# A graph-attention kernel on one core: the fourth unit of tile 0 joined to the third by VectorE, the folds of one unit moved from GpSimd to VectorE, and a new order

## The chip, the cores and the metric

The kernel runs on one core of a Trainium2 chip. The metric is the device time of one launch in microseconds (us). The kernel before has a median of 1622.75 us over three runs (1618.98 to 1625.38); one more execution was profiled.

The engines are named as the profile names them: PE is TensorE's matmuls and PEld its weight loads, DVE is VectorE, ACT is ScalarE, POOL is GpSimd, SP is SyncE, which only issues DMAs here. A small q behind a name is the engine's sequencer. L1356 is line 1356 of the kernel.

## The reference

One layer of masked attention over a graph, behind a layer norm. `x` has 16 batches of 1024 rows of 512 numbers, `adj` is one 1024 x 1024 matrix for all batches, and there are 8 heads of 64.

```python
h = jnp.maximum(_layernorm(x, axis=-1), 0.0)
q = (h @ Wq + bq).reshape(b, n, H, HD)          # k and v likewise
scores = jnp.einsum('bihd,bjhd->bhij', q, k) / jnp.sqrt(jnp.float32(HD))
mask = jnp.where(adj == 0, jnp.float32(-1000000000.0), jnp.float32(0.0))
scores = scores + mask[None, None, :, :]
weights = jax.nn.softmax(scores, axis=-1)
out = jnp.einsum('bhij,bjhd->bihd', weights, v)
x = x + out.reshape(b, n, H * HD)
```

All of it is fp32. The inputs' `adj` is sparse, with few long rows and many short ones, so most scores are masked.

## The kernel before, in words

**The gather.** The kernel doesn't compute the masked scores. Once, at the start, it sorts the 1024 rows by their number of neighbours and makes for each row a list of its neighbours. The sorted rows form eight tiles of 128 rows (one row in a partition): tile 0 has the longest lists, up to 11 neighbours, tile 7 the shortest, 2 (`CAPS`). Rows with still more neighbours have the rest in "pieces" of four, 128 pieces in one tile of their own, called -1. For each batch the kernel computes k and v of all rows, stores them in DRAM (`store_kv`), and gathers for each slot of a list the k and v rows with one indirect DMA that GpSimd issues (L1288). A row's own k and v come with a direct DMA by SyncE instead (L1286, "own rows").

**Units.** A tile's slots are worked off in units of two to four slots, 14 a batch. Their numbers: 0 is tile 7, 1 tile 6, 2 tile 5 (written (5, 0): tile and first slot), 3 tile 4, 4 and 5 tile 3, 6 and 7 tile 2, 8 and 9 tile 1. Tile 0 has four: unit 10 is (0, 0), unit 11 the pieces (-1, 0), unit 12 (0, 4), unit 13 (0, 8) with three slots. A unit has one of six buffers (`g`) from its first gather to its last use, and the buffers go round in the units' order. In each unit:

- VectorE multiplies the gathered k by the query, which is in PSUM (`multiply`, L1298), and adds up each head (`score`, L1302);
- ScalarE takes the exponential (`exponent`, L1306);
- the v rows are weighted by it, most slots on ScalarE (`weigh_s`, L1332: eight small instructions, one for each head), one of some units on VectorE (`weigh_v`, L1318);
- the weighted slots are added together by `fold` (L1337), on VectorE or GpSimd. Of four slots the first step adds two slots to two and the second one to one; of three slots both steps add one to one. `fold_on_pool` sends a step of one slot to GpSimd if the unit is listed in `POOL_FOLDS`.

Units of the tiles 1 to 7 end on VectorE: `join` (L1344) adds the second unit of a tile to its first, and `scale` (L1392) or the shared weights divide by the sum of the exponentials. Tile 0 is added up on TensorE: `add_up` (L1356) multiplies what the folds left with the identity (`ident`), for the pieces with a matrix that gives each piece to its row (`owner_t`), all into one PSUM tile. In fp32 one such call is two matmul instructions in the profile. `residual` adds x (L1406), and GpSimd issues the scattered store (`put_out`, L1409).

**The other half.** For the next batch, in between: `load_x`, `stats`, `power`, `norm`, transposes on TensorE (`flip`) and copies by ScalarE (`unflip`), the projections (`proj_kv` and `queries`, L1057: four calls or eight instructions each), and their evictions by ScalarE (L1075) or VectorE (L1073). The queries of tile 0 are also copied by ScalarE to SBUF (`copy_q`, L1279), from where TensorE makes the pieces' queries (L1275).

**What sets the order.** Each engine runs its instructions in the order in which they are written. `planned` lists every operation with its engine, the operations before it and the buffers it uses; `PLACES` has a place for each (once, for the first k and v, for batches 0, 1, 2, for all from 3 on, for the last but one and for the last), to which `PERIOD` times the batch is added. `ordered` sorts each engine's queue by place and merges the queues. Waits are then put in by the data and buffers that the instructions share. In the last batch the units come in the order `LAST_ORDER`, tile 0 first, and other lists say which engine does what.

Of the kernel before, what the change touches and what calls it, by code (L numbers as in the profile page):

```python
# [57 lines left out]
UNITS = tuple(unit for t in TILES for unit in PARTS[t])  # L58
# [8 lines left out]
POOL_FOLDS = ((5, 0), (4, 0), (1, 0), (1, 4), (-1, 0))  # L67
# [6 lines left out]
LAST_BY_VECTOR = {(2, 0): 0, (2, 3): 0, (0, 0): 0, (-1, 0): 0, (3, 0): 0, (1, 4): 0}  # L74
VECTOR_RESIDUAL = (4,)
LAST_VECTOR_RESIDUAL = (5, 4, 6, 7)
# [21 lines left out]
        list_of=(-13.2, -13.4, 13.93, 14.05, -4.33, -7.76, -9.88, 14.25,),  # L98
        tell=(-12.63, -16.97, -13.14, 9.24, 0.89, 16.11, 17.75, 19.88,),
        spread=(45.38, 47.45, 30.7, 45.48, 45.35, 30.46, 22.54, 45.26,),  # L100
        collect=(-9.17, 5.02,),
        others=(14.42,),
        perm_of=(0.42,),
        spots=(26.84,),
        long_rows=(30.4,),
        long_blocks=(16.58, 20.59, 22.61, 24.22, 24.98,),
        longest=(27.18, 29.37, 32.28, 35.43, 36.11, 39.52, 41.52, 44.79, 45.14,),
        count_pieces=(46.89,),
        first_piece=(122.72,),
        owners=(94.07,),  # L110
        flip_owners=(136.43,),
        copy_owners=(113.68,),
        list_pieces=(137.27,),
        pieces=(127.38,),
        slots=(142.24,),
        add_bias=(-19.2, -17.6,),
        spread_bias=(68.07,),
        copy_bias=(89.7,),
# [4 lines left out]
        norm=(75.49, 76.09, 77.09, 77.49, 79.89, 80.09, 80.34, 80.69,),  # L123
        flip=(75.49, 75.69, 76.49, 76.69, 78.69, 78.89, 90.39, 104.64,),
        unflip=(75.89, 76.49, 77.29, 77.89, 80.49, 80.72, 96.22, 97.88,),
        proj_kv=(75.89, 77.49, 76.29, 77.89, 76.89, 78.49, 79.09, 79.29, 86.87, 98.15, 99.79, 107.75, 135.06, 147.6, 153,
            148.32,),
        evict_kv=(76.89, 79.29, 77.69, 79.49, 78.09, 80.29, 80.4, 80.66, 96.1, 96.13, 96.42, 106.28, 154.55, 162.49, 169.71,
            172.46,),
        store_kv=(78.35, 116.17, 119.38, 125.35, 140.7, 146.55, 148.18, 147.06,),  # L130
        variance=(75.89, 76.89, 79.29, 81.69,),
        power=(75.69, 76.29, 78.29, 87.8,),
# [3 lines left out]
        load_x=(30.09, 30.5, 38.8, 45.21, 45.44, 47.92, 49.07, 49.69,),  # L136
        norm=(2.13, 2.31, 24.77, 49.09, 71.39, 77.14, 77.27, 78.66,),
        flip=(50.32, 51.95, 54.11, 55.9, 60.64, 67.45, 67.52, 68.48,),
        unflip=(27.69, 53.06, 72.64, 77.2, 79.54, 81.13, 82.77, 84.23,),
        queries=(67.49, 69.07, 115.56, 126.07, 127.49, 138.29, 148.67, 168.76, 169.97,),  # L140
        gather=(45.09, 65.92, 63.96, 81.66, 82.98, 67.8, 87.05, 86.63, 69.01, 87.14, 102.98, 103.26, 67.61, 108.86, 109.63,
            108.64, 107.92, 79.49, 116.69, 119.1, 130.36, 131.45, 130.44, 102.76, 142.21, 138.67, 142.4, 144.98, 150.63,
            142.37, 142.46, 108, 152.91, 152.09, 152.7, 153.37, 153.1, 152.82, 153.23, 171.08, 171.84, 155.19, 172.79,
            155.41, 171.17, 171.11,),
        multiply=(47.46, 64.59, 81.01, 107.03, 126.74, 113.33, 126.77, 141.63, 149.43, 155.18, 163.45, 170.22, 180.88,
            178.07,),
        score=(47.54, 67.41, 96.06, 111.76, 129.2, 117.87, 128.06, 146.83, 153.31, 155.84, 165.66, 174.39, 181.78, 195.93,),
        exponent=(92.19, 93.82, 105.44, 111.15, 115.51, 115.42, 115.56, 141.97, 143.4, 152.67, 166.31, 172.53, 173.27,
            183.23,),
        row_sums=(64.37, 70.18, 97.04, 118.27, 142.77, 160.52, 163.48, 203.64,),  # L150
        share=(64.49, 74.75, 101.56, 119.16,),
        weigh_v=(69.44, 130.54, 142.01, 144.6, 161.03, 163.57, 170.25, 175.36, 195.82,),
        weigh_s=(92.85, 101.83, 100.44, 95.75, 106.78, 112.94, 106.75, 115.48, 115.39, 115.45, 122.29, 116.89, 121.19, 119.7,
            142.94, 135.53, 142.97, 143.03, 144.58, 154.99, 152.31, 153.27, 163.13, 166.52, 165.91, 171.8, 172.93, 171.74,
            173.08, 173.04, 172.99, 174.92, 175.62, 181.86, 185.22, 185.42, 187.44,),
        fold=(71.91, 97.01, 97.07, 132.47, 137.68, 138.95, 141.69, 143.23, 145.64, 143.05, 153.79, 155.15, 156.82, 161,
            163.76, 171.2, 173.85, 175.66, 181.17, 186.5, 187.92, 183.84, 200, 202.21, 204.35, 204.53,),
        residual=(109.25, 124.53, 138.45, 141.77, 153.19, 171.14, 178.55, 219.35,),
        put_out=(129.95, 130.51, 141.35, 142.43, 153.4, 178.16, 179.5, 225.23,),
        join=(147.89, 161.06, 175.01,),  # L160
        scale=(148.16, 161.67, 176.53, 211.41,),
        copy_q=(145.23,),
        add_up=(188.54, 194.88, 203.87, 205.55,),
        more=(201.41,),
# [212 lines left out]
PAIRED = ()  # L377
# [1230 lines left out]
```

## Time and profile before

| | |
|---|---|
| median of three runs (lowest, highest) | 1622.75 us (1618.98, 1625.38) |
| profiled execution: its time, its span | 1612.02 us, 1609.9 us |
| mean granted TensorE clock | 0.992 |
| busy, share of the span: PE, DVE, ACT, POOL | 98%, 94%, 90%, 78% |
| DMA: moved, mean over the span | 531.56 MB, 330 GB/s |
| L1356, sums of tile 0 on TensorE: with `ident`, with `owner_t` | 170 and 38 matmul instructions |
| L1337, folds: on VectorE, on GpSimd | 301 and 90 |
| L1344, joins on VectorE | 45 |
| L1406, residuals: on GpSimd, on VectorE | 109 and 19 |

Busy time is the union of an engine's instructions. The shares are means over a start (the sorting and the first batch, to about 100 us), a steady part, and the last batch (from about 1500 us). A wait is written as who waited, "<-", and what came last of what it waited for; the releaser is inferred.

### The profile page before, as it was taken

How to read it: one execution, taken by the hardware profiler on the slowest of the kernel's cores; microseconds unless marked ns; L12 is line 12 of the kernel's file. 1: busy time of each engine (PE TensorE's matmuls, PEld its weight loads, DVE VectorE, ACT ScalarE, POOL GpSimd, SP SyncE). 2: the span in 40 equal slices, each digit the busy share in tenths (PEclk: the TensorE clock that was granted, in tenths of full speed). 3: DMA queues.
4: the chain of work that ended last, by engine and by line, in shares of the span. 5: the costliest groups of instructions: out<-in, count | busy, mean ns of one | idle time of the engine just before them, and what ended most of it. 6: DMA issues, size and time to landing. Idle time of an engine off the chain costs nothing. (4 is left out here: it accounts for less than half of the span.)

```text
span 1609.9 us, 19515 instructions
## 1 busy us (share of the span) xinstructions
PE 1572.1 (98%) x4242; PEld 732.0 (45%) x4242; DVE 1518.2 (94%) x2075; ACT 1444.8 (90%) x5428; POOL 1258.7 (78%) x1185
## 2 busy tenths in 40 slices
PE   8999999999999999999999999999999999999687
PEld 4444444444444444444444444444444444444233
DVE  8889999999999999999999999999999999999897
ACT  4459999898999989899898989999998998989897
POOL 3777778887788888888788787878788887786666
PEclk9999999999999999999999999999999999999899
DMA  6499989999999999999999999999999999998886
GB/s 249 141 351 341 334 319 358 329 366 323 341 333 345 366 333 357 325 351 349 339 357 346 345 337 345 344 343 352 330 339 331 341 373 326 338 335 330 324 306 217
DMA packets 149876, 531.56 MB, mean 330 GB/s; under 512 B 19052, under 2 KB 19052, under 8 KB 149752
## 3 DMA queue, kind: packets, MB, share of 16 engines
q0 software_dynamic: 109840, 390.70, 67.9%
q1 hardware_dynamic: 39912, 139.56, 23.0%
q8 instruction: 35, 0.57, 0.1%
q14 instruction: 89, 0.73, 0.1%
HBM read 429.46 MB, written 100.72 MB: 329 GB/s over the span
## 5 line engine op out<-in xcount | busy, mean ns | idle before, releaser
L1332 ACT ACTIVATE g<-g,weights 128x64 f32<-128x64 f32 x4704 | 1160.3, 338 | 40.9 <-DVE weights L1311 37.8
L1288 POOL DMA_INDIRECT g<-kv,index x608 | 642.2, 1056 | 206.7 <-issue 163.2
L1057 PE MATMUL pq<-wq,hT 128*128 128x512 f32 x1024 | 462.4, 595 | 0.0
L1057 PE MATMUL pk<-wk,hT 128*128 128x512 f32 x960 | 431.7, 593 | 0.0
L1057 PE MATMUL pv<-wv,hT 128*128 128x512 f32 x960 | 431.4, 593 | 0.0
L1302 DVE TENSOR_REDUCE weights<-g 128x32 f32<-128x2048 f32 (+2 forms) x224 | 423.7, 1897 | 2.0
L1298 DVE TENSOR_TENSOR g<-g,pq 128x2048 f32<-128x2048 f32 (+2 forms) x208 | 388.7, 1870 | 28.1 <-DMA g<-kv 9.9
L1057 PEld LDWEIGHTS pq<-wq,hT 128*128 128x128 f32 x1024 | 195.8, 191 | 216.9 <-issue 213.2
L1057 PEld LDWEIGHTS pv<-wv,hT 128*128 128x128 f32 x960 | 182.4, 190 | 213.5 <-issue 210.6
L1057 PEld LDWEIGHTS pk<-wk,hT 128*128 128x128 f32 x960 | 182.7, 190 | 201.4 <-issue 196.8
L1337 DVE TENSOR_TENSOR g<-g 128x512 f32<-128x512 f32 (+1 forms) x301 | 253.9, 851 | 9.8 <-ACT g L1332 8.4
L1409 POOL DMA_INDIRECT out_dram<-x,perm x128 | 136.7, 1068 | 39.8 <-issue 30.6
L1002 POOL DMA_INDIRECT x<-in_x_dram,perm x128 | 135.8, 1061 | 34.9 <-issue 32.5
L1337 POOL TENSOR_TENSOR g<-g 128x512 f32<-128x512 f32 x90 | 115.0, 1284 | 17.6 <-DVE g L1337 10.5
L1037 ACT ACTIVATE h<-x,shift,rstd 128x512 f32<-128x512 f32 x120 | 96.5, 807 | 12.0 <-DVE shift L1027 11.4
L1318 DVE TENSOR_TENSOR g<-g,weights 128x512 f32<-128x512 f32 x143 | 101.9, 716 | 1.1 <-ACT weights L1306 0.6
L1356 PE MATMUL acc<-g,ident 128*128 128x512 f32 x170 | 84.4, 612 | 14.6 <-ACT g L1332 10.8
L1044 PEld LDWEIGHTS pht<-ident,h 128*128 128x128 f32 x512 | 63.2, 141 | 68.6 <-issue 52.7
L1406 POOL TENSOR_TENSOR x<-x,o 128x512 f32<-128x512 f32 x64 | 81.9, 1280 | 9.4 <-DVE o L1392 5.0
L1049 ACT COPY hT<-pht 128x512 f32<-128x512 f32 x128 | 73.0, 571 | 16.3 <-PE pht L1044 16.2
L1011 DVE BATCH_NORM_STATS2 st<-x 128x6 f32<-128x512 f32 x120 | 81.2, 677 | 1.6 <-DMA x<-in_x_dram,perm 1.6
L1044 PE MATMUL pht<-ident,h 128*128 128x128 f32 x512 | 76.5, 273 | 3.2 <-ACT hT L1049 1.9
(242 smaller groups left out, 1080.2 us busy)
## 6 DMA issues: line engine op xcount, KB each, us to landing
g<-kv SPq DMA_DIRECT2D x128, 512.0 KB, 7.7
kv<-kvt SPq DMA_DIRECT2D x120, 512.0 KB, 6.9
g<-kv,index POOLq DMA_INDIRECT x608, 6.9
adj<-in_adj_dram SPq DMA_DIRECT2D x8, 512.0 KB, 8.2
x_first<-in_x_dram SPq DMA_DIRECT2D x8, 256.0 KB, 6.0
x<-in_x_dram,perm POOLq DMA_INDIRECT x128, 5.5
out_dram<-x,perm POOLq DMA_INDIRECT x128, 6.6
wk<-in_L_gnn_Wk_dram SPq DMA_DIRECT2D x1, 1024.0 KB
```

The source lines that it names most:

```text
L1002: nc.gpsimd.indirect_dma_start(out=X[n][:], out_offset=None, in_=x_rows, in_offset=on(ap=perm[:, t : t + 1], axis=0), element_offset=b * N * D
L1037: nc.scalar.activation(HN[n], X[n], AF.Relu, bias=shift, scale=scale)
L1044: nc.tensor.transpose(PH[n][:, c, :], hn[:, ts(c, P)], ident)
L1057: nc.tensor.matmul(pt, HT[n][:, c, :], W[name][:, c, :], start=(apart and c == 0), stop=(n != -NT and c == DC - 1))
L1288: nc.gpsimd.indirect_dma_start(out=G[i][:, s].rearrange("p j d -> p (j d)"), out_offset=None, in_=KV[b % len(KV)][:], in_offset=on(ap=inde ...
L1298: nc.vector.tensor_tensor(k, k, Q[b, t][:, None, :].to_broadcast([P, count, D]), ALU.mult)
L1302: nc.vector.tensor_reduce(weights[:, w, :], heads(G[i][:, :count, 0, :]), AX.X, ALU.add)
L1318: nc.vector.tensor_tensor(v, v, own.to_broadcast([P, n, H, HD]), ALU.mult)
L1332: nc.scalar.activation(v[:, h, :], v[:, h, :], AF.Identity, scale=weights[:, c + s, h : h + 1])
L1337: engine.tensor_tensor(v[:, 0:n], v[:, 0:n], v[:, first : first + n], ALU.add)
L1356: nc.tensor.matmul(ACC[b, home], owner_t if t < 0 else ident, v[:, s, :], start=(u == added_up(b, B, home)[0] and s == 0), stop=(u == adde ...
L1409: nc.gpsimd.indirect_dma_start(out=out_rows[t], out_offset=on(ap=perm[:, t : t + 1], axis=0), in_=X.pop(b * NT + TILES.index(t))[:], in_of ...
```

## The change

1. `PAIRED = (13,)`: in all batches but the last, unit 13 isn't added up by TensorE. VectorE adds what its folds left to what unit 12's folds left (`join`), and `add_up` of unit 12 comes after that. TensorE's sum of unit 13 is gone.
2. (5, 0) is taken out of `POOL_FOLDS`: the folds of unit 2 run on VectorE in all batches but the last.
3. In the plan, the products with tile 0's queries come after `copy_q`.
4. All of `PLACES` is new, but for the setting up; `PERIOD` is not. The numbers of `gather` run through the units' slots: 2, 3, 3, 4, 3 for the units 0 to 4, each unit's own rows first, so the ninth is unit 3's own rows and the thirteenth unit 4's.
5. Names for choices of the last but one and last batch are added (`NEXT_BY_VECTOR`, `NEXT_VECTOR_RESIDUAL`, `LAST_BIAS_V`), with the values that hold already, so that nothing else moves between engines.

```diff
-POOL_FOLDS = ((5, 0), (4, 0), (1, 0), (1, 4), (-1, 0))
+POOL_FOLDS = ((4, 0), (1, 0), (1, 4), (-1, 0))
...
+NEXT_BY_VECTOR = {}
 VECTOR_RESIDUAL = (4,)
+NEXT_VECTOR_RESIDUAL = (4,)
...
     3: dict(
...
-        gather=(81.3, 95.92, 84.77, 96.24, 101.5, 93.61, 104.18, 105.24, 124.06, 105.69, 105.83, 105.64, 118.16, 106.87,
...
+        gather=(66.07, 89.24, 70.01, 91.38, 100.4, 76.39, 101.46, 101.42, 76.42, 103.76, 103.83, 103.73, 83.49, 109.7,
...
-        multiply=(104.31, 108.38, 121.3, 125.25, 127.41, 132.1, 133.56, 142.79, 159.17, 169.72, 175.28, 177.26, 181.52,
-            184.87,),
+        multiply=(104.25, 110.59, 119.84, 125.39, 135.7, 135.76, 142.58, 145.92, 158.62, 170.51, 176.28, 178.06, 182.5,
+            186.22,),
...
-        join=(156.53, 173.11, 182.2,),
+        join=(156.45, 172.06, 182.71, 207.03,),
...
-        add_up=(198.74, 209.02, 213.28, 217.7,),
+        add_up=(197.16, 207.42, 220.85,),
...
     'last': dict(
...
-        multiply=(309.74, 279.38, 229.66, 203.14, 192.6, 203.5, 167.97, 183.01, 166.51, 168.83, 118.21, 127.6, 139.29,
-            140.78,),
+        multiply=(316.24, 246.56, 244.49, 216.36, 215.21, 219.95, 166.24, 186.15, 163.23, 169.42, 128.78, 142.19, 148.77,
+            150.02,),
...
-        copy_q=(115.48,),
+        copy_q=(113.43,),
...
 BIAS_V = {0: 'DVE', 2: 'DVE', 4: 'DVE', 6: 'DVE'}
-PAIRED = ()
+LAST_BIAS_V = BIAS_V
+PAIRED = (13,)
...
-        add(("multiply", k), "DVE", slots + [q_of[q]], [g, q])
+        add(("multiply", k), "DVE", slots + [q_of[q]] + ([("copy_q", b)] if t == 0 else []), [g, q])
...
 def residual_by_vector(b, B, t):
-    return t in (VECTOR_RESIDUAL if b < B - 1 else LAST_VECTOR_RESIDUAL)
+    return t in (LAST_VECTOR_RESIDUAL if b == B - 1 else NEXT_VECTOR_RESIDUAL if b == B - 2 else VECTOR_RESIDUAL)
...
-def bias_by(n, name):
+def bias_by(n, name, B):
 
-    return BIAS_V.get(n % NT, "PE") if n >= 0 and name == "v" else "PE"
+    kinds = LAST_BIAS_V if n >= (B - 1) * NT else BIAS_V
+    return kinds.get(n % NT, "PE") if n >= 0 and name == "v" else "PE"
```

The functions that the change calls and that were there before, `pairs_up`, `added_up`, `folds` and `fold_on_pool`, and the branch of `planned` for paired units:

```python
        elif pairs_up(b, B, u):
            add(("join", k), "DVE", weighed + earlier, [g, ("g", k - 1)])
            plan.ops[plan.number["add_up", k - 1]][2].append(("join", k))
            added = [("add_up", b * NU + v) for v in added_up(b, B, home)]
```

## The prediction

> **What bounds the kernel now.** I read the engine totals first, then the busy time by stretch, then who waits for whom in the steady stretch, then the timeline of its two ends. Two rows of the busy time by stretch (columns: length, then the busy time of PE, PEld, DVE, ACT and POOL with their instruction counts, the granted clock, the DMA share, GB/s), the first the steady part, the second the last batch with the drain:
>
> ```profile
> 400.00:1300.00 900.00, 899.16 (x2431) 419.88 (x2431) 865.00 (x1114) 851.32 (x3232) 737.30 (x676) 1.00 0.95 344
> ...
> 1500.00:1610.00 110.00, 81.83 (x186) 34.47 (x184) 89.57 (x102) 89.22 (x372) 68.45 (x66) 0.90 0.77 277
> ```
>
> In the steady part TensorE is busy 899.2 of 900 us at full clock. That it is really full, and not only drawn full, shows in the weight loads: inside one projection they follow at a fixed step, so one fp32 matmul instruction of 512 columns takes 0.43 us of the engine whatever its modelled length (0.59) says.
>
> ```profile
> 802.38 0.19 PEld L1057 LDWEIGHTS pk<-wk,hT 128*128 128x128 f32 x1 [0.24 <-issue]
> 802.81 0.19 PEld L1057 LDWEIGHTS pk<-wk,hT 128*128 128x128 f32 x1 [0.24 <-issue]
> ```
>
> The batch period is the distance of the same matmul in consecutive batches: the pieces' query starts at 440.6 in one batch and at 1008.6 six batches later, so 568.0 / 6 = 94.67 us. TensorE sets it. Right behind is VectorE, 865.0 of 900 busy. Its 35.0 us of idle time are 26.0 us of waits, the four largest kinds of which follow (who waits for whom, us, times, longest), and 9.0 us of short gaps between instructions, which I take as fixed:
>
> ```profile
> DVE g L1298 <- DMA g<-kv: 9.2, 9, 1.7
> DVE g L1337 <- ACT g L1332: 3.2, 9, 0.4
> DVE g L1298 <- PE pq L1057: 3.2, 5, 0.6
> DVE kvt L1073 <- PE pv L1057: 2.7, 5, 0.9
> ```
>
> 900 us are 9.51 batches, so VectorE waits 2.73 us a batch and otherwise needs 94.67 - 2.73 = 91.94 us. ScalarE (851) and GpSimd (737) have more room.
>
> **The change, part by part.**
>
> *One sum leaves TensorE.* For a paired unit `add_up` isn't planned at all. In the steady part line L1356 runs 54 matmuls with `ident` in nine batches, 6 a batch for three units, so one unit's sum is 2 instructions, 2 x 0.43 = 0.86 us. Fifteen batches (all but the last): 12.9 us. TensorE's period would be 93.81 us.
>
> *Three sums come to VectorE.* The price of each is this row (busy time, then mean ns); the second row is what a GpSimd sum takes:
>
> ```profile
> L1337 DVE TENSOR_TENSOR g<-g 128x512 f32<-128x512 f32 x135 | 91.1, 685 | 3.8 <-ACT g L1332 3.2
> ...
> L1337 POOL TENSOR_TENSOR g<-g 128x512 f32<-128x512 f32 x57 | 72.6, 1281 | 6.0 <-ACT weights L1306 2.1 <-ACT g L1332 1.5 <-issue 0.8
> ```
>
> The join is one. The "one fold" is two: unit (5, 0) has three slots, `folds` gives it two steps of one slot each, and `fold_on_pool` sends every step of one slot of a listed unit to GpSimd. (The 90 GpSimd folds of the run are 15 batches x 6, where five units with one each would make 75.) So 3 x 0.685 = 2.05 us a batch, 30.8 us in all, join included, and VectorE needs 91.94 + 2.05 = 93.99 us: as much as TensorE's new 93.81. GpSimd is relieved of 2 x 1.28 = 2.56 us a batch; it was at 82%, so I cost that at nothing.
>
> *What period comes out.* The lower end is 93.99, with no wait left on VectorE. Of its 2.73 us of waits, 0.83 are for TensorE's queries, projections and sums (3.2 + 2.7 + 2.0 us in the window) and these shrink when TensorE is no longer the slower one. 0.97 (9.2 us) are for unit 3's own rows, and these are held up by an order that the new tables turn round, as rival B's rows show. The other 0.94 us wait for ScalarE, GpSimd and gathers, mostly 0.3 to 0.6 us at a time, less than the 2.05 us by which VectorE now comes later. If all of the 0.94 stay the period is 94.93. I take a third, 0.31: 94.30, or 0.37 x 15 = 5.5 us less. If all of today's waits stay it is 96.7; both ends go into the range.
>
> *GpSimd's sums blocking VectorE's.* Sums that meet are seen. One weighting of 0.68 us takes 1.58 us beside a fold on GpSimd, and ends 0.56 us after that one does:
>
> ```profile
> 985.64 1.28 POOL L1337 TENSOR_TENSOR g<-g 128x512 f32<-128x512 f32 x1
> ...
> 985.90 1.58 DVE L1318 TENSOR_TENSOR g<-g,weights 128x512 f32<-128x512 f32 x1
> ```
>
> VectorE's products with a query in PSUM aren't lengthened (2.28 us with and without). Added over 400 to 1300, ten VectorE instructions are longer than the median of their form, by 5.7 us against 124 GpSimd sums, 0.046 us for each. Two sums fewer a batch give 30 x 0.046 = 1.4 us at that rate. Three more exposed sums a batch, with an order found anew, can cost the same; 5.7 / 9.51 = 0.6 us a batch (9 us) is what is to be gained at most, and as much again is my bound for a loss. I take nothing. The Trainium skill (SBUF — State Buffer, "Who interferes with whom") says that a VectorE instruction with two SBUF inputs and a GpSimd one that reads SBUF exclude each other for a whole instruction; by that alone the two folds removed would be worth up to 30 x 1.28 = 38 us, an estimate from the row above with every one of them in the way. The rows say that the order already keeps nearly all of them apart. Against the change stands another page of the Trainium skill (Perfetto Trace Analysis, "Optimizing Scalar/DVE Operations"): it advises to move work off a saturated VectorE, and doubts that moving it between VectorE and GpSimd helps; by it nothing of the above would be won.
>
> *The last batch.* Planning the product of tile 0 after `copy_q` adds no instruction and no wait; both read the same query, and the trace shows that the product waits for the copy already:
>
> ```profile
> 1524.34 0.56 ACT L1279 COPY q<-pq 128x512 f32<-128x512 f32 x1
> ...
> 1524.93 2.29 DVE L1298 TENSOR_TENSOR g<-g,pq 128x2048 f32<-128x2048 f32 x1 [4.98 <-ACT q L1279]
> ```
>
> The old plan took the product to be free to run, while the copy stood behind ScalarE's weighting. VectorE lost 4.98 us, and ScalarE's next exponential, waiting for these scores, began after 4.67 idle us. In this stretch these two are the fullest (89.6 and 89.2 of 110), and TensorE has room (81.8). With the dependency known, the new tables put the product further behind the copy (15.4 where it was 2.7). I take the whole 5.0 us as gone. What is late next is the gather of that unit's rows, so 0 is the other end.
>
> *Everything else in the order.* All places are new. Outside 100 to 1500 us VectorE idles 20.4 us of the last 110, and TensorE 7.4 us of the first 100. New order there may win some 8 us of these or put back one or two stalls of 5 us. I take nothing, and give the range these ends.
>
> *The sum*, against the profiled execution (span 1609.9, with what lies around it 1612.0): 1612.0 - 5.5 - 5.0 = 1601.5. The median shown, 1622.75, is 10.7 above that execution; I keep the offset: 1612.2, so 1612, or 0.7% less.
>
> **The rivals.** A difference of 0.5%, 8.1 us, is about what a measurement of this kernel can tell from none.
>
> *A, TensorE still sets the period.* VectorE's waits vanish and its lengthened sums too, so all of 12.9 us arrives, with the tail's 5.0: 1612.0 - 17.9 + 10.7 = 1605. For it: TensorE is without gaps today beside a VectorE at 96%. Against it: 93.99 is above 93.81 already.
>
> *B, slower: a buffer comes free later, and VectorE is the bound.* Unit 12's buffer is freed by its sum on TensorE (the first row), and goes to unit 4 of the next batch. That sum must now wait for unit 13's folds and join, so it can come no earlier than unit 13's own sum did (the second row):
>
> ```profile
> 859.86 1.02 PE L1356 MATMUL acc<-g,ident 128*128 128x512 f32 x2
> ...
> 864.37 1.02 PE L1356 MATMUL acc<-g,ident 128*128 128x512 f32 x2
> ...
> 871.74 2.29 DVE L1298 TENSOR_TENSOR g<-g,pq 128x2048 f32<-128x2048 f32 x1 [1.43 <-DMA g<-kv]
> ```
>
> Today SP waits for it with unit 4's own rows (issued at 860.96), and unit 3's own rows, whose buffer had been free since the pieces' sum at 855.9, stand behind them (861.44, landed at 871.62); so VectorE waits 1.43 us for unit 3. In the new tables for batches from 3 on unit 3's own rows come first (76.42 against 83.49; 124.06 and 118.16 before). That speaks for the change. But unit 4's two gathers on GpSimd, with all that is queued behind them there, and the stores on SP behind unit 4's own rows, now wait until 864.4 plus the join's 0.69 at least: 4.2 us more than 860.9. Against it: unit 4's product starts at 878.0, its place has moved back by 8.3 us, and two GpSimd folds are gone. If the 0.94 us of other waits stay and a quarter of the 4.2 reaches VectorE, the period is 93.99 + 0.94 + 1.05 = 95.98, 19.7 us more in fifteen batches, less the tail's 5.0: 1637. It decides when over 1.55 us of waits a batch are left (0.68 of room, and 13.1 / 15 = 0.87).
>
> *C, nothing to see.* VectorE at 94.6 keeps the period and the tail's stall only moves to the next gather: 1612.0 - 0 to 5, so 1618 to 1623. That the sum isn't taken off TensorE can be ruled out from the plan.
>
> **How the numbers follow.** The forecast's case 0.40 (its own range 1604 to 1620, three fifths of it below 1614.6), A 0.19, C 0.18, B 0.23. Faster: 0.24 + 0.19 = 0.43; same: 0.16 and 0.16 of C, 0.32; slower: B and the rest of C, 0.25. The range goes from A with 8 us of a better order, 1597, to just past B, 1638.
>
> **What would show it.** L1356 with `ident` at 140 matmuls for 170, L1344 at 60 for 45, L1337 at 331 on VectorE and 60 on GpSimd. Period near 94.3, VectorE over 97.5% and TensorE at 99 to 100% in the steady part; no wait for `copy_q` near 5 us in the last batch. I am wrong if the period is at or over 94.7 (B or C; B shows as VectorE waiting for gathered or own rows in units 4 and after), or if the tail keeps its length without that stall.

## The result and the profile after

The changed kernel takes 1631.3 us (median of 6 runs, 1626.9 to 1635.1) where the kernel before takes 1623.15 us on the same chip: a ratio of 1.005 (95% interval 1.0035 to 1.0066). Measured once more on another chip with more runs (`a_again` below) the ratio is 1.0029 (1.0016 to 1.0042). So it is slower, by 0.3 to 0.5%, where 0.7% less was forecast.

Busy time by stretch in the kernel after (columns: length, busy time of PE, PEld, DVE, ACT and POOL with their instructions, granted clock, DMA share, GB/s), the steady part and the last batch with the drain:

```profile
400.00:1300.00 900.00, 897.79 (x2429) 418.16 (x2428) 875.51 (x1161) 850.65 (x3236) 716.83 (x663) 1.00 0.95 346
1500.00:1626.00 126.00, 98.97 (x218) 41.62 (x216) 102.77 (x112) 99.96 (x412) 74.34 (x72) 0.87 0.73 267
```

TensorE is still full in the steady part, and VectorE has gained 10.5 us of work in 900 and still has 24.5 us of idle time. The groups of instructions show that the operations did what the change says: 140 matmul instructions with `ident` (170 before), 331 folds on VectorE and 60 on GpSimd, and 60 joins (45 before).

```profile
L1358 PE MATMUL acc<-g,ident 128*128 128x512 f32 x140 | 71.5, 630 | 10.2 <-ACT weights L1308 5.6 <-DVE g L1320 1.5 <-ACT g L1334 1.2
...
L1339 DVE TENSOR_TENSOR g<-g 128x512 f32<-128x512 f32 (+1 forms) x331 | 269.6, 826 | 2.6 <-ACT g L1334 1.2
...
L1339 POOL TENSOR_TENSOR g<-g 128x512 f32<-128x512 f32 x60 | 76.6, 1277 | 11.8 <-DVE g L1339 9.4
...
L1346 DVE TENSOR_TENSOR g<-g,g 128x512 f32<-128x512 f32 x60 | 40.5, 675 | 0.1
```

VectorE's waits in the steady part (us, times, longest), of the kernel after: the 9.2 us for unit 3's own rows are gone, and no kind of wait as large has taken their place. All together fell from 26.0 to 17.0 us; four of the largest kinds are:

```profile
DVE g L1300 <- issue: 4.9, 5, 1.4
DVE g L1300 <- DMA g<-kv,index: 4.0, 3, 2.6
DVE g L1300 <- PE pv L1059: 3.2, 2, 1.7
DVE kvt L1075 <- PE pk L1059: 1.6, 1, 1.6
```

**Where the time went.** The steady part did get faster; the start and the end got slower by more. This is best seen with TensorE as the clock. The two profiles compared here are one execution each and come from chips on which the kernel before has the same median (1615.1 and 1615.0): `b_again`, the kernel before unchanged (span 1609.0), and `a_again`, the kernel after unchanged (span 1619.6). The cuts are the pieces' query of batch 0, of batch 3 and of batch 12. First the kernel before:

```profile
0.00:155.00 155.00, 144.95 (x430) 70.81 (x434) 135.68 (x325) 90.75 (x252) 103.32 (x123) 1.00 0.74 265
155.00:440.60 285.60, 284.28 (x763) 132.13 (x769) 273.87 (x352) 269.42 (x1028) 230.19 (x211) 1.00 0.93 339
440.60:1294.00 853.40, 851.12 (x2289) 397.79 (x2306) 817.60 (x1057) 804.62 (x3056) 694.49 (x641) 1.00 0.95 344
1294.00:1609.00 315.00, 287.83 (x735) 129.99 (x738) 286.76 (x344) 279.98 (x1096) 228.18 (x213) 0.96 0.88 318
```

and the kernel after:

```profile
0.00:162.20 162.20, 151.54 (x445) 73.46 (x446) 140.77 (x334) 95.47 (x265) 105.81 (x124) 0.99 0.73 262
162.20:453.60 291.40, 283.55 (x763) 130.68 (x762) 280.91 (x363) 268.00 (x1024) 224.46 (x205) 1.00 0.92 333
453.60:1300.90 847.30, 844.88 (x2288) 392.88 (x2287) 823.16 (x1082) 802.03 (x3052) 680.28 (x622) 1.00 0.96 346
1300.90:1619.60 318.70, 285.56 (x721) 127.45 (x719) 286.54 (x345) 278.44 (x1089) 222.66 (x207) 0.95 0.86 310
```

The nine steady periods take 6.1 us less. Setup takes 7.2 more, batches 0 to 2 take 5.8 more, the rest takes 3.7 more: +10.6 in all. (The medians on one chip differ by only 5.6 us, 1620.5 and 1615.0: the execution of `b_again` lies 3.9 us under the median of its chip, so a few microseconds of the +10.6 are not the change's.) The second number of each row set against the first is TensorE's idle time. It is the same in the steady part (2.3 and 2.4 us), but 7.9 for 1.3 us in batches 0 to 2 and 33.1 for 27.2 us at the end. The weight loads (the PEld counts, of which no record is missing) say how much of a difference is work that only moved across a cut. (They are taken here by their starts; the rows count one that straddles a cut on both sides.) Before the first cut the kernel after does 8 projection matmuls, one matmul for the bias and 4 transposes more (8 x 0.43 + 0.22 + 4 x 0.11 = 4.1 us; the bias and four transposes stand at 0.22 and 0.44 us in the chain of waits), and in the last stretch it does as many fewer, and 6 matmul instructions of sums fewer (6.7 us). Beyond its work, then, setup loses 7.2 - 4.1 = 3.1 us, batches 0 to 2 lose 5.8 + 2.6 (their 6 instructions of sums saved) = 8.4 us, the steady part 7.7 - 6.1 = 1.6 us, and the end 3.7 + 6.7 = 10.4 us. That is 23.5 us against the 12.9 us of sums saved.

Who TensorE waits for in batches 0 to 2 (us, times, longest): in the kernel after (`a_again`),

```profile
PE pk L1057 <- ACT kvt L1077: 4.1, 3, 2.0
PE acc L1358 <- POOL g L1339: 1.6, 1, 1.6
PE pq L1057 <- DVE g L1300: 1.3, 2, 0.7
```

where the kernel before has one wait, of 0.8 us. None of these waits is for the join (L1346), and in the last stretch only 1.3 of `a_again`'s 33.1 idle us are. At the end, the chain of waits of the first profile of the kernel after, in order of time (start, length, what), goes through two gathers, an issue and a load of own rows, 33 us together:

```profile
1525.57 5.68 DMA g<-kv,index
...
1541.28 9.46 DMA g<-kv,index
...
1580.02 8.76 issue
1589.63 9.31 DMA g<-kv
```

The three loads stand in the chain of `a_again` too (24.8 us), the issue does not. The chain of the kernel before goes back only to 1596.7 us, so the two can't be set side by side.

### The profile page after: what moved, and what is told of

It reads as the page before. It is cut to its first block, busy times and chain, and to the rows that moved or that the text cites. A ratio compares the mean times of both kernels' runs of the same rounds, so it can differ in the third digit from the quotient of the medians.

```text
span 1625.1 us, 19439 instructions
## 1 busy us (share of the span) xinstructions
PE 1568.2 (96%) x4212; PEld 727.5 (45%) x4212; DVE 1530.5 (94%) x2120; ACT 1444.0 (89%) x5428; POOL 1223.2 (75%) x1155
## 5 line engine op out<-in xcount | busy, mean ns | idle before, releaser
L1290 POOL DMA_INDIRECT g<-kv,index x608 | 634.9, 1044 | 229.7 <-issue 167.8
L1300 DVE TENSOR_TENSOR g<-g,pq 128x1536 f32<-128x1536 f32 (+2 forms) x208 | 388.5, 1870 | 31.2 <-DMA g<-kv,index 17.4
L1339 DVE TENSOR_TENSOR g<-g 128x512 f32<-128x512 f32 (+1 forms) x331 | 269.6, 826 | 2.6 <-ACT g L1334 1.2
L1411 POOL DMA_INDIRECT out_dram<-x,perm x128 | 142.8, 1116 | 45.5 <-issue 34.5
L1046 PE MATMUL pht<-ident,h 128*128 128x128 f32 x512 | 75.7, 275 | 13.3 <-ACT h L1039 10.5
L1339 POOL TENSOR_TENSOR g<-g 128x512 f32<-128x512 f32 x60 | 76.6, 1277 | 11.8 <-DVE g L1339 9.4
L1308 ACT ACTIVATE weights<-weights 128x32 f32<-128x32 f32 (+2 forms) x224 | 48.3, 219 | 39.3 <-DVE weights L1304 32.0
L1358 PE MATMUL acc<-g,ident 128*128 128x512 f32 x140 | 71.5, 630 | 10.2 <-ACT weights L1308 5.6
```

Source lines behind the costliest of these rows:

```text
L1046: nc.tensor.transpose(PH[n][:, c, :], hn[:, ts(c, P)], ident)
L1290: nc.gpsimd.indirect_dma_start(out=G[i][:, s].rearrange("p j d -> p (j d)"), out_offset=None, in_=KV[b % len(KV)][:], in_offset=on(ap=inde ...
L1300: nc.vector.tensor_tensor(k, k, Q[b, t][:, None, :].to_broadcast([P, count, D]), ALU.mult)
L1339: engine.tensor_tensor(v[:, 0:n], v[:, 0:n], v[:, first : first + n], ALU.add)
L1358: nc.tensor.matmul(ACC[b, home], owner_t if t < 0 else ident, v[:, s, :], start=(u == added_up(b, B, home)[0] and s == 0), stop=(u == adde ...
L1411: nc.gpsimd.indirect_dma_start(out=out_rows[t], out_offset=on(ap=perm[:, t : t + 1], axis=0), in_=X.pop(b * NT + TILES.index(t))[:], in_of ...
```

## The experiments

The theory after the result: TensorE sets the period, so its removed sum brings what the steady part gained, and the loss is in the order made for the start and the end. (The runs bore out the first half, and of the second only setup.) Rival: the three sums on VectorE (or their waits) cost the time wherever they stand. Where a kernel takes places from both versions, a step whose turn would lock the order is put ahead of what stood before it; the number of such steps is given.

### Each kernel again, unchanged: b_again, a_again

> The kernel before, unchanged, profiled once more, because its first profile (1612.0 us) lies 11 us under its median. Theory S (the start): the pieces' query of batch 3 starts near 441 us again, and the 11 us are lost in one place in or behind the start, so the loss of the changed kernel in its start (19 us between the two profiles) is smaller between typical executions, 8 to 19 us. Theory O (the operations): the 11 us are spread over the batches, a period of 95.3 us for 94.66, and the changed kernel's period of 94.1 us isn't much of a gain.

> The kernel after unchanged, beside the kernel before on one chip. Theory (the start of the new order loses what the steady part gains): the query of the pieces of batch 3 comes 13 to 20 us later than before's, the periods from batch 3 to batch 12 are 93.8 to 94.2 us, the last batch needs about 3 us more; ratio 1.003 to 1.007. If the slow stretch of 8 us at 76 to 86 us of the first profile was of that execution alone, the slots of the first list take about 3 us here and the start loses 13 us rather than 19. Rival (the steady part did not gain; the periods differ by chip or execution): periods of 94.7 us here too.

`b_again`: 1611.2 us in one execution, with the same times at the same marks as the first profile within 1.4 us. It too lies under its chip's median (by 3.9 us), so it does not show where the 11 us between the first profile and its median went. `a_again`: 1620.5 us, ratio 1.0029 (1.0016 to 1.0042), periods 93.79 to 94.79 in the steady part, batch 3 at 453.6 us for 440.6. In the first profile of the kernel after a slow stretch at 76 to 86 us added some 8 us to the start; it does not recur (the slots of the first list take 2.9 us here and took 10.7 there). The theory's numbers hold, but for single periods and a ratio at the edge: the start loses 13 us, the steady part gains 6, the end loses 4.

### Is TensorE the clock? pe_back and sum_out

```diff
 # pe_back: the kernel after, the sum of the paired unit counted twice
+                if u == 12 and b < B - 1:
+                    nc.tensor.matmul(ACC[b, home], ident, v[:, s, :], start=False, stop=False)
                 nc.tensor.matmul(
 # sum_out: the kernel before, in add_up (the stop flag goes to the unit ahead)
+            if u == 13 and b < B - 1:
+                return
```

> The kernel after in its own order, with one more TensorE sum in each batch but the last: the sum of tile 0's third unit is counted twice, so TensorE has again the two matmul instructions of 0.43 us that the change took from it, and VectorE's work is as in after (tile 0's output counts that unit twice). Theory (TensorE sets the period, and its removed sum is the gain): the period goes from 93.8 to 94.65 us, 12 to 13 us more in all, ratio to after 1.007 to 1.009. Rival (the gain is from the order alone, which keeps waits off): under 3 us more.

> The kernel before in its own order, with the TensorE sum of tile 0's fourth unit left out in every batch but the last and nothing put in its place (tile 0's output lacks that unit): TensorE has 30 matmul instructions of 0.43 us less, VectorE and GpSimd work as in before. Theory (TensorE sets the period in any order; what the change lost is in the start and the end of the new order): start and end as in before, the steady period 93.8 us for 94.7, 11 to 13 us less in all, ratio 0.992 to 0.993. Rival (before's order has waits of VectorE that come to light when TensorE is shorter): 2 to 7 us less.

`pe_back` takes 1629.2 us beside 1620.5 for the kernel after: 8.7 us or 0.5% more, under the theory's 0.7 to 0.9% and over the rival's 3 us. The pieces' query, per matmul tile (count, shortest/median/longest ns, first and last start): the kernel after,

```profile
L1277 PE MATMUL pq_-1_5457<-q,owner x2: 592/594/595, 642.1 to 642.6; 128*128 128x512 f32 x2
L1277 PE MATMUL pq_-1_6270<-q,owner x2: 592/594/595, 736.1 to 736.5; 128*128 128x512 f32 x2
L1277 PE MATMUL pq_-1_7083<-q,owner x2: 592/594/595, 829.8 to 830.3; 128*128 128x512 f32 x2
L1277 PE MATMUL pq_-1_7896<-q,owner x2: 592/594/595, 923.6 to 924.1; 128*128 128x512 f32 x2
```

and `pe_back`:

```profile
L1277 PE MATMUL pq_-1_6276<-q,owner x2: 592/594/595, 736.9 to 737.3; 128*128 128x512 f32 x2
L1277 PE MATMUL pq_-1_7090<-q,owner x2: 592/594/595, 831.5 to 831.9; 128*128 128x512 f32 x2
L1277 PE MATMUL pq_-1_7904<-q,owner x2: 592/594/595, 926.2 to 926.6; 128*128 128x512 f32 x2
```

Five of the nine steady periods of the kernel after are 93.8 or 93.9 us, seven of those of `pe_back` 94.6 or 94.7, and the kernels differ by two matmul instructions a batch and nothing else: TensorE sets the period after the change as it did before. All nine steady periods together take 852.6 us for 847.3, so 5.3 of the 7.7 us come through there.

`sum_out` is the most that the removed sum can give, since nothing pays for it: 1607.75 us, ratio 0.9961 (0.9946 to 0.9975), 6.3 us less, between the theory's and the rival's numbers. Its nine steady periods take 847.4 us (853.4 before), as many as the changed kernel's 847.3, and its stretch after batch 12's query takes 319.0 us for 315.0. So of the 12.9 us half comes through: the steady part gives 6.0 of its 7.7, and the end, which should give 2.6, takes 4.0. The rows of these two stretches:

```profile
437.80:1285.20 847.40, 845.46 (x2288) 393.79 (x2287) 819.74 (x1056) 802.94 (x3056) 699.86 (x641) 1.00 0.96 346
1285.20:1604.20 319.00, 286.83 (x734) 129.49 (x732) 287.24 (x345) 281.12 (x1100) 228.82 (x214) 0.96 0.88 315
```

At the end TensorE waits for ScalarE, GpSimd and VectorE (11.9, 3.6 and 3.8 us at the sums, for 9.8, 2.8 and 3.8 in `b_again`), so a shorter TensorE waits longer. Why the stretch grows by 4.0 us is open, but it does so in before's own order and without any work added to VectorE: a loss of the size that the changed kernel has there (318.7 us) needs no new order.

### Has VectorE room? join_twice

```diff
 # the kernel after, in join
-            nc.vector.tensor_tensor(first, first, G.pop(i)[:, 0, 1, :], ALU.add)
+            last = G.pop(i)[:, 0, 1, :]
+            for _ in range(2 if i % NU in PAIRED else 1):
+                nc.vector.tensor_tensor(first, first, last, ALU.add)
```

> The kernel after in its own order, with the sum that joins the fourth unit to the third made twice (tile 0's output counts the fourth unit twice): 0.685 us more of VectorE in each batch, at the place of the change. Theory (TensorE sets the period and VectorE's neighbouring instructions overlap, so that it has some 1.5 us of room in each batch): under 4 us more in all. Rival (VectorE is the engine that decides, at 93.99 us of need by the prediction's sum): the period grows by 0.6 to 0.7 us, 9 to 10 us more in all.

1618.7 us for 1620.5, steady periods 93.79 to 94.75, nine of them 846.5 us for 847.3. A fourth sum in each batch costs nothing. VectorE does not decide, though the prediction's sum had it full with three.

### Is it the order? Tables of before with the operations of after: ops_only, head2_old, tail_old

```diff
 # the kernel after; PLACES of these stages from the kernel before, with the join
 # behind the fourth unit's folds and the third unit's sum at the fourth's old place
 # ops_only:  all stages              (27 steps put ahead)
 # head2_old: setup, first, 0, 1, 2   (10)
 # tail_old:  next, last              (14)
```

> The changed kernel's operations (unit 13 joined by VectorE, unit 2's folds on VectorE) in the order of before; the new join stands right behind unit 13's folds, unit 12's sum takes the place of unit 13's old one, and 27 operations are pulled ahead where the old order can't hold them. Theory S: the start is that of before, so it isn't slower by what the changed kernel is; with an order not made for these sums I expect 1618 to 1628 us for 1623. Theory O: the sums on VectorE cost the time whatever the order: 1631 us or more, with VectorE waiting in every batch.

> The changed kernel with the tables of before for the setting up, the first k and v and the batches 0, 1 and 2 (10 operations pulled ahead at the seam). Theory S: the 15 to 19 us lost before batch 3 come back, less what the seam costs: 1613 to 1619 us, the pieces' query of batch 3 at 440 to 446 us, and a period of 93.8 to 94.2 us behind it. Theory O: no change from 1631 us.

> The changed kernel with the tables of before for the last but one and the last batch (14 operations pulled ahead at the seam). Theory S: the end costs 0 to 5 us, so 1626 to 1632 us. A third theory, E (the end): the new order of the last batch is what lost the time, since from the last pieces' query to the end it takes 95.3 us for 84.8: 1619 to 1623 us.

Ratios 1.035 (1.0332 to 1.0368), 1.0353 (1.0335 to 1.037) and 1.042 (1.0395 to 1.0446). In `ops_only` the steady period is 95.9 us: the operations in the old order, with 27 steps put ahead, lose where the same operations in the new order gain. Its time (1671 us) is theory O's, not S's, but the steps put ahead are part of it. The other two did not isolate anything: at the seam between the two tables the periods are 105 to 122 us in `head2_old` and 133.6 and 118.9 us in `tail_old`. In both the seam costs more than the order could win.

### The start and the end by mixed orders: head_mix, head_later, tail_mix

```diff
 # the kernel after with one list of places: for each step w x (time in before's order)
 # + (1 - w) x (time in after's order, shifted to match); w goes linearly
 # head_mix:   1 to 0 from some 200 to 300 us
 # head_later: 1 to 0 from some 400 to 500 us of that list's time
 # tail_mix:   0 to 1 from some 1300 to 1500 us of that list's time
```

> The kernel after, with its order changed at the start alone: each step's place is a mean of its time in before's order and in after's, before's alone up to some 200 us and after's alone from some 300 us on, with a linear change of weight between, so that there is no seam. Theory (the loss is in the order of the start): the query of the pieces of batch 0 comes at 155 us as in before, the steady periods are 93.8 us, and the time is 5 to 10 us under after's, thus below before's by 0 to 5 us, if the mixed stretch costs under 5 us. Rival (the start's loss comes from the operations: the third of tile 0's sums or the two folds on VectorE delay the first batches in any order): the pieces of batch 3 come 13 us late again and the time stays at after's.

> The kernel after with before's places up to some 380 us of the run, so for the setup and batches 0 to 2, after's from some 470 us on, and a mean with changing weight between. Theory (after's order of the start loses 10 us, half of it in TensorE's waits in batches 0 to 2; before's order of the same operations does not): the query of the pieces of batch 2 comes at 350 to 352 us, the mixed stretch costs 2 to 5 us, then periods of 93.8; time 4 to 9 us under after's. Rival (the three sums on VectorE need another order from batch 0 on): the first periods are 96 us and more, time at after's.

> The kernel after with its own places up to some 1250 us, before's from some 1450 us on (most of batch 14 and the last batch), and a mean with changing weight between. Theory (the end of after's order costs 12 us beyond its work, with clock and waits; before's order of the end costs less): from the query of the pieces of batch 12 to the end 313 to 317 us for after's 318.7, time 2 to 5 us under after's. Rival (what is late at the end comes from the batches ahead of it, or the mixed stretch costs more than the end gives): 318 us or more, time at after's or above.

No step had to be put ahead in these. `head_mix`: 1618.0 us, ratio 1.0027 (1.0012 to 1.0042), not told apart from the kernel after. Its query of batch 0 comes at 155.0 us, as before the change, and that of `a_again`, on the same chip, at 162.2:

```profile
L1387 PE MATMUL pq_-1_1358<-q,owner x2: 592/592/592, 155.0 to 155.4; 128*128 128x512 f32 x2
```

```profile
L1277 PE MATMUL pq_-1_1444<-q,owner x2: 592/592/592, 162.2 to 162.6; 128*128 128x512 f32 x2
```

So the 7 us of setup were the order's and no operation's. But batches 0 to 2 then take 294.0 us, 101.5 of them in the mixed batch. `head_later`: 1621.35 us, ratio 1.0045; 155.8 us, then 96.2, 100.8 and 101.2 us. The first two of these periods are in before's places, where the kernel before takes 94.8 and 99.8 us with a sum more on TensorE: the new operations cost some 2 us there without the new order, and the rival's numbers (96 us and more, time at after's) came out. The mixed stretch costs more still. `tail_mix`: 1624.9 us, ratio 1.0059; 322.8 us from batch 12's query to the end, for 318.7. For the end, too, the rival's numbers came out. None of the three beats the kernel before.

### The fold: fold_back and fold_only

```diff
 # fold_back: the kernel after        (40 steps put ahead, most of them folds)
-POOL_FOLDS = ((4, 0), (1, 0), (1, 4), (-1, 0))
+POOL_FOLDS = ((5, 0), (4, 0), (1, 0), (1, 4), (-1, 0))
 # fold_only: the kernel before       (27 steps put ahead, the same as in ops_only)
-POOL_FOLDS = ((5, 0), (4, 0), (1, 0), (1, 4), (-1, 0))
+POOL_FOLDS = ((4, 0), (1, 0), (1, 4), (-1, 0))
```

> The kernel after with the two folds of the unit at tile 5 back on GpSimd, in after's places (where GpSimd's queue would lock, the fold goes ahead of what stood before it): VectorE has 1.37 us less in each batch, GpSimd some 3 us more. Theory (VectorE has room, the move of this fold neither gains nor costs in the steady part): steady periods 93.8 to 94.2, time within 4 us of after's. Rival 1 (VectorE's work costs time): 5 us or more under after's. Rival 2 (GpSimd's sums hold VectorE's up and its gathers come later): 5 us or more above after's.

> The second part of the change alone: the kernel before with the two folds of the unit at tile 5 on VectorE, at the places that they had on GpSimd (27 steps are taken ahead where the order would lock), TensorE's work as before. Theory (a fold put into VectorE's queue at GpSimd's time stands ahead of work that others wait for, so it asks for a new order): periods of 95.5 to 96 us as with both parts in before's order, 30 us or more above before. Rival (both parts share that loss, the join made half of it): under 20 us above before.

`fold_back`: 1663.5 us, 43 us above the kernel after's 1620.5 on a chip of the same level; the theory here missed, rival 2 has it. The nine steady periods take 858.9 us for 847.3, so most of the loss is at the start and the end. In the steady part VectorE waits for GpSimd's folds (line L1339 of after is L1383 there), ten times in nine batches:

```profile
DVE x L1452 <- POOL g L1383: 20.9, 10, 3.1
DVE g L1344 <- PE pht L1090: 8.0, 5, 2.0
```

`fold_only`: ratio 1.0198 (1.0156 to 1.0241), the first periods 104.5 and 107.9, then 95 to 96.5, as its theory said. Moved without a new order the fold loses in both directions, and no run shows a gain from it. Neither run prices the fold itself: both carry steps put ahead.

### The join alone in before's order: join_only and join_mid

```diff
 # the kernel before with PAIRED = (13,): the join behind the fourth unit's folds, the
 # third unit's sum at the fourth's place; every other step keeps its place on its engine
 # join_mid: additionally
-    return b < B - 1 and u in PAIRED
+    return 3 <= b < B - 2 and u in PAIRED
```

> The first part of the change alone: the kernel before with tile 0's fourth unit joined to the third by VectorE, its sum by TensorE gone, the two folds of the unit at tile 5 on GpSimd as before, and before's order of every other step on each engine; the join stands on VectorE right behind the fourth unit's folds, the third unit's TensorE sum at the place that the fourth's had. Theory (TensorE sets the period, VectorE has room, and before's start and end stay): start 155, steady periods 93.8 to 94.3 as with the sum left out, 3 to 7 us under before, ratio 0.996 to 0.998. Rival (the third unit's buffer is freed some 8 us later and its next gathers land late, the prediction's rival B): VectorE waits for gathers in units 4 of the batches, periods of 95 us and more, over 3 us above before.

> The join alone in before's order, as join_only, but only in batches 3 to 13, which is where TensorE did not wait for it there; in batches 0, 1, 2 and 14 the fourth unit is summed by TensorE as in before. Theory (the join costs only where TensorE arrives at the sum before VectorE has made the join: 0.9 to 1.8 us in each of batches 0 to 2 and 5.1 us in batch 14, with what follows from it): start and end as in before, periods of 93.8 to 94.3 between, 4 to 7 us under before, ratio 0.9955 to 0.9975, as with the sum left out. Rival (the join's 0.685 us and the third unit's later buffer cost the steady batches more than TensorE's 0.86 us brings): same as before or slower, ratio 1.000 to 1.005.

`join_only`: ratio 1.0096 (1.0061 to 1.013), slower than the rival of the expectation asked, but not by its mechanism: VectorE waits 4.9 us in all for gathers in 860 us of the steady part (own rows included). Instead TensorE arrives at the third unit's sum before VectorE has made the join. Its waits for the join are 0.95, 0.92 and 1.80 us in batches 0, 1 and 2 and 5.10 us in batch 14, and none over 0.7 us in between. The timeline of `join_only` (start, length, instruction, idle time before and what ended it; its L1389 and L1401 are after's L1346 and L1358):

```profile
404.60 0.69 DVE L1389 TENSOR_TENSOR g<-g,g 128x512 f32<-128x512 f32 x1
...
405.35 1.13 PE L1401 MATMUL acc<-g,ident 128*128 128x512 f32 x2 [1.80 <-DVE g L1389]
```

```profile
1561.60 2.29 DVE L1343 TENSOR_TENSOR g<-g,pq 128x2048 f32<-128x2048 f32 x1 [4.97 <-ACT q L1324]
1563.92 2.29 DVE L1347 TENSOR_REDUCE weights<-g 128x32 f32<-128x2048 f32 x1
1566.12 1.89 DVE L1382 TENSOR_TENSOR g<-g 128x512 f32<-128x512 f32 x3
1568.04 0.69 DVE L1389 TENSOR_TENSOR g<-g,g 128x512 f32<-128x512 f32 x1
...
1568.79 2.07 PE L1401 MATMUL acc<-g,ident 128*128 128x512 f32 x2 [5.10 <-DVE g L1389]
```

The second fence shows how a join lengthens a stall that was there already: VectorE waits for the copied query, makes that product first, and only then the folds and the join that TensorE stands for.

`join_mid`, without the join in just these batches, still has a ratio of 1.0051 (1.0024 to 1.0079): about half of `join_only`'s loss is gone, the other half is not, so the rival has that half. Its profile has one wait of TensorE for the join between 440 and 1320 us, of 1.0 us, which is not the 8 us. Why they stay is open. These two runs, `fold_only` and the runs with an earlier copy were made on two chips where the kernel before takes 1635.6 and 1635.75 us, and single profiles there show waits that the profile can only call "remote" (12.8 us of TensorE's in `join_only` between 440 and 1300 us; `b_again` and `a_again` have none), so their steady periods can't be compared one by one.

### The stall of the last batch: copy_early, join_copy, mid_copy

```diff
 # last batch, the copy two weighing steps earlier on ScalarE
-        copy_q=(115.48,),
+        copy_q=(110.9,),
```

> The kernel before with one step moved: in the last batch ScalarE copies the query (copy_q) two weighing steps of 2.03 us earlier, when TensorE has just made it; the two steps come after it. Theory (the 5.0 us that VectorE waits at 1519 us is a stall on the path to the end): 3 to 4 us under before, ratio 0.998. Rival (the last gathers, whose buffers and descriptors come at their own time, set the end): within 1 us of before; VectorE's wait shows again as waits for gathers.

> The kernel before with the join alone (as join_only) and the earlier copy of the last query (as copy_early) together. Theory: both gains add, 6 to 10 us under before, ratio 0.994 to 0.996, and the fastest kernel of the study. Rival (what the steady part gains is waited for at the end): no better than join_only.

> join_mid with the last batch's copy of the query two weighing steps earlier, as in copy_early. Theory: both gains add, 7 to 11 us under before, ratio 0.993 to 0.9955, the fastest of the study. Rival (the end waits for gathers whatever comes before it): within 1 us of join_mid.

`copy_early` is the fastest kernel of this study that does the whole work: ratio 0.997 (0.9947 to 0.9994), about 5 us under before (the interval reaches from 1 to 9 us), one number changed. VectorE's 5.0 us wait is gone and small waits stand in its place (us, times, longest, from 1500 us to the end):

```profile
DVE g L1298 <- issue: 1.8, 3, 0.8
DVE g L1298 <- DMA g<-kv,index: 1.5, 2, 0.8
DVE sums L1378 <- ACT weights L1306: 1.3, 2, 0.8
DVE g L1298 <- ACT g L1332: 1.2, 1, 1.2
```

On top of the join the same edit makes the ratio 1.0075 for 1.0096 and 1.0033 for 1.0051, each 0.2% less. The intervals of these pairs overlap, so the two agree with the gain but don't prove it by themselves; and the forecast that either would beat the kernel before missed.

`join_copy` beside `copy_early` also shows what the join alone costs in before's order. They ran on the same chip, and in the traces every engine runs the same instructions in the same order but for 15 joins more on VectorE and 15 sums (30 matmul instructions) less on TensorE. The medians are 1648.0 and 1630.3 us: 17.7 us more. Batches 0 to 2 and the stretch after batch 12's query, first of `copy_early`:

```profile
162.90:450.30 287.40, 284.62 (x762) 131.90 (x768) 274.86 (x352) 269.44 (x1030) 227.68 (x211) 1.00 0.93 338
1323.90:1637.20 313.30, 288.31 (x735) 130.40 (x738) 288.52 (x345) 281.81 (x1104) 228.47 (x213) 0.96 0.89 316
```

and of `join_copy`:

```profile
163.20:456.20 293.00, 285.17 (x756) 131.21 (x762) 282.62 (x355) 268.89 (x1024) 228.18 (x211) 0.99 0.93 333
1324.90:1645.90 321.00, 288.49 (x729) 129.71 (x732) 293.05 (x349) 282.25 (x1104) 228.88 (x214) 0.95 0.87 312
```

The join makes these two stretches longer by 5.6 and 7.7 us, where the whole change made them longer by 5.8 and 3.7. These are single profiles (that of `copy_early` is of its slowest execution, 1639.4 us), on a chip with the "remote" waits, but they take the ground from the view that the new order must be what lost there.

## Why the prediction was wrong, point by point

- **The step that failed is "Everything else in the order. All places are new … I take nothing", and with it the gain of 0.37 us taken for all fifteen batches.** The term was given bounds of -8 and +10 us and put at nothing. The steady part did gain, but setup takes 7.2 us more for 0, batches 0 to 2 take 5.8 us more where 1.1 less was counted, and the stretch after batch 12's query 3.7 us more where 6.1 less was. That setup's part is the order's alone is shown (`head_mix` has batch 0's query at 155.0 us with the new operations). For the other two it stays open how much is the new order's and how much the join's: in before's own order the join alone makes them 5.6 and 7.7 us longer (`join_copy` beside `copy_early`), and the sum left out without a join already makes the last one 4.0 us longer (`sum_out`). The prediction read 400 to 1300 us closely and the other 700 us of a 1610 us run by two idle totals.
- **"The last batch … I take the whole 5.0 us as gone": the stall went, the time did not.** The price fits: taken away by itself the stall is worth about 5 us (`copy_early`, 1 to 9). In the first profile of the changed kernel VectorE has no wait for `copy_q` in the last batch, but from 1495 us on waits 6.1 us for gathers, 5.5 us at one of them, and 1.9 us for own rows. The prediction named this ("what is late next is the gather of that unit's rows, so 0 is the other end") and took the good end.
- **Period: 94.30 forecast, 94.14 measured (847.3 / 9), 94.82 before. Near in size, wrong in reason.** The gain was 0.68 us a batch for 0.37 forecast. The sum had VectorE full at 93.99 us. In fact TensorE still sets 93.8 (`pe_back`, `join_twice`), as rival A said of the steady part. The price of 2.05 us for three sums was too high: over the nine steady periods VectorE's busy time grew by 5.6 us (817.60 to 823.16 in the rows above), 0.62 us a batch. Neighbouring VectorE instructions overlap in the records: over eight steady batches of the first two profiles the durations grew by 12.6 us but the time that they cover only by 3.5 us (727.0 to 730.4; 14.2 and 6.1 us between `b_again` and `a_again`), while the waits fell from 23.0 to 14.5 us.
- **"TensorE's period would be 93.81 us", for 12.9 us in all: right as a limit, half as a gain.** Left out at no cost, the sum brings 6.3 us (`sum_out`), so rival A, which had all 12.9 us arrive, failed as well.
- **GpSimd's blocking, taken at nothing:** over eight steady batches, the VectorE instructions beside a GpSimd sum that are over 0.1 us longer than their form's median are 10 (5.7 us) and 3 (3.0 us) in the two profiles of the kernel before, and 3 (2.4 us) and 2 (2.2 us) in those of the kernel after. The same kernel's two profiles differ by nearly as much as the two kernels do, so a gain is not shown; nothing was a fair price. The Trainium skill (SBUF — State Buffer, "Who interferes with whom") has a rule by which up to 38 us were to be had, by the prediction's estimate; 0.8 to 3.3 us in eight batches are what the runs show.
- **Rival B, the buffer:** not what made it slower. The wait for own rows (9.2 us) is gone, as the part that speaks for the change said, and gathers cost VectorE 4.0 us in 900.
- **The views named to show it:** 140, 60, 331 and 60 as foretold, VectorE at 97.3% (875.5 of 900; over 97.5% was expected), TensorE at 99.8%, no wait for the copy. Of the signs of error the last came true: "the tail keeps its length without that stall".
- **The sum by stretches,** forecast (0.37 us for each batch, 5.0 at the end) and measured between `b_again` and `a_again`: setup 0 and +7.2; batches 0 to 2 -1.1 and +5.8; the nine steady periods -3.3 and -6.1; the rest -6.1 and +3.7. Together -10.5 and +10.6 us.

## What to carry to other kernels

Price a new order of places for the start, the steady part and the end apart, with the bound engine's idle time and its instruction counts at the same marks, before taking a steady gain of 0.7 us a batch as the answer. When work leaves the bound engine and a later result of another engine takes its place, look in every stage for who arrives first; in the stages where the other engine is behind, the sum saved becomes a wait (`join_only`). A loss found beside a new order need not be the order's: add the operation alone to the old order, and compare stretch by stretch. A stall that one number can take away (a short copy behind long work on an in-order engine) is worth trying by itself before it is counted as a part of a larger change.

## What the runs showed of the hardware

- VectorE's instructions of one kind overlap in the records: three folds of 0.685 us in a row cover 1.89 us, so one behind another takes 0.60 us. Adding durations overstates what a full engine needs.
- TensorE's granted clock was lower where TensorE was less busy: 0.87 in the last 126 us of the kernel after (99.0 us busy), 1.00 in the steady part (897.8 of 900). Work may look longer at a lower clock; that would fit that the end of `a_again` does 6.7 us less of TensorE's work than that of `b_again` in only 2.3 us less of busy time, at clocks of 0.95 and 0.96. No run separates the two.
- The same program differs between chips by more than the change is worth: the kernel before has medians of 1614 to 1636 us on the chips used here, so only ratios on one chip tell versions apart.
